# Turning the softmax of an attention layer: TensorE transposes against transfers between SBUF quarters and a 32x32 block transpose

## The chip, the core and the metric

The kernel runs on one core of a Trainium2 chip. The metric is the device time of one execution in microseconds (us). A core has TensorE (PE in the profile, with its weight loads as PEld), VectorE (DVE), ScalarE (ACT), GpSimd (POOL) and SyncE (SP), whose queue issues most of the transfers. Each engine takes its instructions strictly in the order in which they stand in its queue.

## The reference, cut to what matters

The program is a graph layer followed by a transformer block with gated mixtures in its attention, on N = 1250 nodes of D = 1024 features, H = 16 heads of P = 64, E = 8 experts of which 2 are chosen. All is float32.

```python
x = x + gnn(layernorm(x), edges, W, b)
z = layernorm(x)
q = rope(einsum('bsd,hdp->bhsp', z, Wq));  k = rope(einsum('bsd,hdp->bhsp', z, Wk))
gv = gate(z, Wsel_v);                      go = gate(z, Wsel_o)
v   = einsum('bsd,bhse,hedp->bhsp', z, gv, Wv)
att = softmax(einsum('bhsp,bhtp->bhst', q, k) / sqrt(P), axis=-1)
o   = einsum('bhst,bhtp->bhsp', att, v)
s1  = layernorm(z + einsum('bhsp,bhse,hepd->bsd', o, go, Wo))
x   = x + layernorm(s1 + relu(s1 @ W1 + b1) @ W2 + b2)
```

The einsum for o sums over the keys t. TensorE sums over partitions, so the attention weights, which come out of the softmax with queries on partitions and keys along the row, have to be turned: keys onto partitions.

## The kernel before, in words

float32 products are made from split operands: `hi` is the operand rounded to a matmul type (a cast on ACT), `lo` the rest (a subtraction on DVE or POOL), and `dot` (L137) adds hi*hi, hi*lo and lo*hi, three matmuls. Weights are read by `weights` (L119): a 128x1024 block into one of two `w_raw` buffers, cast on ACT (L127), rest on POOL (L129), into a ring of five pairs of `w_hi` and `w_lo` during the attention.

The kernel runs through five stages. The graph layer ends near 320 us. `queries_keys` (L558) makes q and k for head after head, about 365 to 600 us, and writes them to DRAM tensors `kq_d` (L594, L596), from buffers of which there are two per part. Then `values` and `attention` run side by side until about 1925 us; `outputs` runs beside the last head's attention until about 2125 us and alone until about 3000 us; `feed_forward` ends the program.

`values` (L704) makes v of one head in 10 tiles of 125 nodes. A tile is 4 steps of 6 matmuls of 512 columns, then on DVE a product with the gate (L717) and a sum over experts (L720), a cast on ACT (L722) and a rest on POOL (L723). The four weight blocks of a head serve one step each: step 1 of every tile uses block 0, step 4 block 3. A block of the next head can be cast only when a pair of the ring is free, which for blocks 1 to 3 is after the same head's last tile has used block 0, 1 or 2.

`attention` (L617) works on chunks of 256 queries, 5 chunks a head, 80 in all; a chunk has two tiles of 128 queries. `softmax` (L622) of a tile: six matmuls into three PSUM banks `s` (one buffer, so the next tile's scores wait until this one's exponentials are made), the maximum over the row on DVE (L637), three exponentials on ACT with sums of their rows (L642), sum, reciprocal and a product with 1/sum on DVE (L645 to L647). `split` (L650), five times a chunk: four TensorE transposes against the identity into a PSUM bank (L655), a cast (L657) and a rest (L659). `product` (L664), five times a chunk: four matmuls with v (L670), all 20 of a chunk summed in one bank. `outputs` (L729) reads o and the output gate (L736, L741) and multiplies by Wo.

The generators are interleaved by hand: after each step of `values` one step of `attention` follows (L834 to L838), and the order on TensorE is kept as written (`manual_schedule`, L832). On the other engines the order is set when the program is built, by a planner that places instructions by its own estimate of when they could start. On the chip the queues follow that order whatever the real times are.

Of the kernel before, what the change touches and what calls it, by code (L numbers as in the profile page):

```python
# [22 lines left out]
N = 1250  # L23
# [13 lines left out]
CUT = NZ * KT  # L37
# [33 lines left out]
def gnn_ffn_kernel(  # L71
# [31 lines left out]
    o_d = [dram.tile([P, N], F32, name=f"o_d{j}") for j in range(NP)]  # L103
    g_d = dram.tile([P, N], F32, name="g_d")
# [61 lines left out]
    def transposed(hi, lo, c0, y, psum_tile):  # L166

        for half in range(2):
            p = psum_tile([P, 4, KT])
            for k in range(4):  # L170
                d0 = (4 * half + k) * P
                nc.tensor.transpose(p[:, k, :], y[:, d0 : d0 + P], ident[:KT, :KT])
            to = (slice(None), slice(4 * half, 4 * half + 4), slice(c0, c0 + KT))
            nc.scalar.copy(hi[to], p)
            nc.vector.tensor_tensor(lo[to], p, hi[to].bitcast(F32), ALU.subtract)
# [8 lines left out]
    with ExitStack() as gctx:  # L184
# [16 lines left out]
        with ExitStack() as bctx:  # L201
# [3 lines left out]
            with tc.tile_pool(name="ring1t", bufs=6) as r1:  # L205
                ring += [r1] * 6

                def prepare(t):
# [10 lines left out]
                    transposed(yh, yl, 0, y[:KT], lambda shape: ps.tile(shape, F32, name="tr2", bufs=2))  # L219
# [274 lines left out]
        zT = [[zpool.tile([P, ND, CUT], F32R, name=f"zT0{k}") for k in range(2)]]  # L494
        for t in range(2, NT):
            new = sums([t])
            if t - 2 < NZ:
                transposed(zT[0][0], zT[0][1], KT * (t - 2), zs.pop(0)[:KT], side_bank)
                zs += new
# [5 lines left out]
    def z_of(t, d):  # L505

        k = t if t < NZ else t - NZ
        return [part[:, d, KT * k : KT * (k + 1)] for part in zT[t >= NZ]]

    def rest_of_z():  # L510

        for t in range(NZ, NT):
            z = raws[0].tile([P, D], F32, name="w_raw")[:KT]
            move(z, z_d[t])
            transposed(zT[1][0], zT[1][1], KT * (t - NZ), z, side_bank)
# [3 lines left out]
    def gates(wpool, tmp):  # L519
# [5 lines left out]
        wide = [KT, 2 * H, NX]  # L525
        order = first_wins[:KT, None, :].to_broadcast(wide)

        def pick(chosen, v, m):

            nc.vector.tensor_reduce(m, v, AX.X, ALU.max)  # L530
# [5 lines left out]
        for t in range(NT):  # L536
            p = side_bank([KT, 2 * P])
# [3 lines left out]
            s, a, b, c = (tmp.tile([KT, 2 * H, NX], F32, name=k) for k in ("s", "a", "b", "chosen"))  # L541
            m = tmp.tile([KT, 2 * H], F32, name="m")
# [5 lines left out]
            nc.vector.tensor_tensor(gate_v[:KT, t, :].rearrange("p (h e) -> p h e", h=H), s[:, :H, :], c[:, :H, :],  # L548
                                    ALU.mult)
            nc.vector.tensor_tensor(a[:, H:, :], s[:, H:, :], c[:, H:, :], ALU.mult)  # L550
            pg = psums[-1].tile([P, KT], F32, name="po", bufs=1)
            nc.tensor.transpose(pg, a[:, H:, :].rearrange("p h e -> p (h e)"), ident[:KT, :KT])
            nc.scalar.copy(gT[:, KT * t : KT * (t + 1)], pg)
# [4 lines left out]
    def queries_keys(tab, work):  # L558
# [9 lines left out]
        chunks = [(0, 0, CUT), (1, 0, 376), (1, 376, N - CUT - 376)]  # L568
# [3 lines left out]
        for h, k in pieces:  # L572
# [19 lines left out]
            if k == 2:  # L592
                for j, part in enumerate((hi.bitcast(F32), lo.bitcast(F32))):
                    nc.sync.dma_start(kq_d[h][HD * j : HD * (j + 1), 0, :], part[HD:])  # L594
# [13 lines left out]
    with tc.tile_pool(name="qktab", bufs=1) as tab, tc.tile_pool(name="qkwork", bufs=2) as work, \  # L608
            tc.tile_pool(name="gatet", bufs=2) as tmp:
        turns, rest = queries_keys(tab, work), rest_of_z()  # L610
        interleave(islice(turns, 2), rest, 1, 1 / 3)
        interleave(turns, gates(tab, tmp), 1, 3)

# [3 lines left out]
    def attention(pool):  # L617


        keys, made = {}, {}  # L620

        def softmax(h, c, i):  # L622
# [5 lines left out]
            q = pool.tile([P, 2, P], F32R, name="q", bufs=4)  # L628
# [8 lines left out]
            nc.vector.tensor_reduce(most, s[:, :, :KW], AX.XY, ALU.max, negate=True)  # L637
            p = pool.tile([P, N], F32, name="p", bufs=5)
            parts = pool.tile([P, 3], F32, name="parts", bufs=4)
            for k, k0 in enumerate(starts):  # L640
                n = KW if k == 2 else KW - 2
                nc.scalar.activation(p[:, k0 : k0 + n], s[:, k, :n], AF.Exp, bias=most,  # L642
                                     accum_out=parts[:, k : k + 1])
            total = pool.tile([P, 1], F32, name="total", bufs=4)
            nc.vector.tensor_reduce(total, parts, AX.X, ALU.add)  # L645
            nc.vector.reciprocal(total, total)
            nc.vector.tensor_scalar_mul(p, p, total)  # L647
            made.setdefault((h, c), []).append(p)

        def split(h, c, k):  # L650

            t = side_bank([KT, 2, QW])
            for j in range(2):
                for i, p in enumerate(made[h, c]):
                    nc.tensor.transpose(t[:, j, P * i : P * (i + 1)], p[:, KT * (k + j) : KT * (k + j + 1)], ident)  # L655
            hi = pool.tile([KT, 2, QW], F32R, name="att_hi", bufs=3)
            nc.scalar.copy(hi, t)  # L657
            lo = pool.tile([KT, 2, QW], F32R, name="att_lo", bufs=3)
            nc.vector.tensor_tensor(lo, t, hi.bitcast(F32), ALU.subtract)  # L659
            return hi, lo  # L660

        sums = {}

        def product(h, c, k, parts):  # L664
            if k == 0:
                sums[h, c] = psums[-1].tile([P, QW], F32, name="po", bufs=1)
            po = sums[h, c]
            for j in range(2):
                for part in parts:
                    nc.tensor.matmul(po, lhsT=v_of[h][:, k + j, :], rhs=part[:, j, :],  # L670
                                     start=(k + j == 0 and part is parts[0]),
                                     stop=(k + j == NT - 1 and part is parts[1]))
            if k + 2 < NT:
                return
# [252 lines left out]
```

## Time and profile before

| | us |
|---|---|
| runs shown (3) | 3124.57, 3132.06, 3143.47; median 3132.06 |
| the profiled execution's own time | 3137.92 |
| its span | 3136.1 |
| PE busy | 3023.9 (96%) |
| PEld, DVE, ACT, POOL busy | 2554.4, 1957.2, 1098.1, 702.2 |
| granted TensorE clock | 0.985 |

The span lies 1.8 us under that execution's time. A row of the groups gives line, engine, operation, what is written and read, count, then busy time and mean duration of one in ns, then the idle time of the engine before these instructions and what ended it. A row of the timeline gives start and length in us, engine, line and operation. Matmuls overlap in the pipeline: the step from one start to the next is what a matmul costs TensorE, and it is shorter than its recorded length.

### The profile page before, as it was taken

Reading aid. Unit: us, or ns where it says so; the run is one execution under the profiler, and the core shown is the slowest. Engines: PE = TensorE matmul, PEld = TensorE weight load, DVE = VectorE, ACT = ScalarE, POOL = GpSimd, SP = SyncE. Lnnn points to the kernel's source line nnn. Section 1 sums busy time; section 2 is a strip of 40 time slices with the busy share of each in tenths; the row PEclk is TensorE's granted clock in tenths of the full one; section 3 lists DMA queues with packets and bytes.
Section 4 is the critical chain, followed back from the end, with each engine's and each line's share of the span. In section 5 each row is a group of like instructions: output and inputs, shape, how many; then the busy total and the mean of one; then the engine's idle time right before and its main releaser. Section 6 shows DMA issues by size and latency. Waiting matters only on the chain. (4 is left out here: it accounts for less than half of the span.)

```text
span 3136.1 us, 41143 instructions
## 1 busy us (share of the span) xinstructions
PE 3023.9 (96%) x15618; PEld 2554.4 (81%) x15618; DVE 1957.2 (62%) x3477; ACT 1098.1 (35%) x2472; POOL 702.2 (22%) x570
## 2 busy tenths in 40 slices
PE   6989899999999999999999999899999999999998
PEld 5777889888888888888888888787777777777787
DVE  7965687566666666666666666664444444444685
ACT  5762323234444444444444444431112112111222
POOL 2000334322222122222212222202112112112223
PEclk9999999999999999999999999999999999999999
DMA  3116555612221121222112122434333333333212
GB/s 111 60 41 190 167 142 160 167 43 52 54 55 37 42 52 47 54 55 53 43 39 53 46 54 54 102 94 123 106 85 98 96 85 103 90 82 109 75 41 92
DMA packets 151825, 254.86 MB, mean 81 GB/s; under 512 B 14521, under 2 KB 111801, under 8 KB 151458
## 3 DMA queue, kind: packets, MB, share of 16 engines
q1 hardware_dynamic: 103934, 210.68, 23.9%
q0 software_dynamic: 45824, 31.22, 5.2%
q10 hardware_dynamic: 1860, 10.24, 1.1%
q8 instruction: 124, 2.03, 0.3%
q14 instruction: 83, 0.68, 0.1%
HBM read 200.25 MB, written 56.96 MB: 82 GB/s over the span
## 5 line engine op out<-in xcount | busy, mean ns | idle before, releaser
L129 POOL TENSOR_TENSOR w_lo<-w_raw,w_hi 128x1024 fp32r<-128x1024 f32 x148 | 372.3, 2525 | 1078.0 <-ACT w_hi L127 1069.6
L141 PE MATMUL mm<-w_hi,go_lo 128*125 128x512 f32 x1280 | 507.6, 399 | 24.6 <-DVE go_lo L750 24.5
L139 PE MATMUL mm<-w_hi,go_hi 128*125 128x512 f32 x1280 | 509.5, 398 | 8.8 <-ACT go_hi L748 7.9
L139 PE MATMUL mm<-w_hi,zT 128*125 128x512 f32 x1280 | 508.4, 397 | 4.6 <-ACT raw L584 4.6
L140 PE MATMUL mm<-w_lo,go_hi 128*125 128x512 f32 x1280 | 509.9, 398 | 0.0
L140 PE MATMUL mm<-w_lo,zT 128*125 128x512 f32 x1280 | 507.1, 396 | 0.1
L141 PE MATMUL mm<-w_hi,zT 128*125 128x512 f32 x1280 | 507.1, 396 | 0.0
L642 ACT ACTIVATE p<-s,most 128x416 f32<-128x416 f32 (+1 forms) x480 | 286.0, 605 | 332.8 <-DVE most L637 329.2
L765 DVE TENSOR_TENSOR acc<-acc,mm 125x512 f32<-125x512 f32 x320 | 217.4, 683 | 163.1 <-PE mm L141 163.1
L659 DVE TENSOR_TENSOR att_lo<-tr,att_hi 125x512 fp32r<-125x512 f32 x400 | 262.6, 685 | 88.7 <-ACT att_hi L657 88.6
L141 PEld LDWEIGHTS mm<-w_hi,go_lo 128*125 128x125 f32 x1280 | 239.9, 187 | 93.6 <-DVE go_lo L750 33.7
L748 ACT CAST go_hi<-gb 128x500 fp32r<-128x500 f32 x160 | 98.2, 614 | 602.2 <-PE mm L140 600.6
L657 ACT CAST att_hi<-tr 125x512 fp32r<-125x512 f32 x400 | 235.1, 589 | 179.0 <-PE tr L655 176.0
L139 PEld LDWEIGHTS mm<-w_hi,go_hi 128*125 128x125 f32 x1280 | 239.9, 187 | 68.3 <-ACT go_hi L748 8.2
L745 DVE TENSOR_TENSOR gb<-gb,oc 128x500 f32<-128x500 f32 x160 | 103.8, 690 | 303.0 <-DMA gb<-g_d 301.8
L141 PEld LDWEIGHTS mm<-w_hi,zT 128*125 128x125 f32 x1280 | 238.3, 186 | 60.5
L140 PEld LDWEIGHTS mm<-w_lo,go_hi 128*125 128x125 f32 x1280 | 239.7, 187 | 58.4
L637 DVE TENSOR_REDUCE most<-s 128x1 f32<-128x1254 f32 x160 | 234.2, 1464 | 81.0 <-PE s L634 80.6
L655 PEld LDWEIGHTS tr<-ident,p 128*125 128x125 f32 x1600 | 234.9, 187 | 53.6 <-DVE att_lo L659 18.6
L139 PEld LDWEIGHTS mm<-w_hi,zT 128*125 128x125 f32 x1280 | 239.1, 187 | 41.0 <-ACT raw L584 4.9
L140 PEld LDWEIGHTS mm<-w_lo,zT 128*125 128x125 f32 x1280 | 239.6, 187 | 36.5 <-POOL w_lo L129 0.4
L655 PE MATMUL tr<-ident,p 128*125 128x128 f32 x1600 | 242.0, 274 | 10.2 <-DVE att_lo L659 8.1
(201 smaller groups left out, 5166.6 us busy)
## 6 DMA issues: line engine op xcount, KB each, us to landing
gb<-g_d SPq DMA_DIRECT2D x160, 250.0 KB
w_raw<-in_wv SPq DMA_DIRECT2D x64, 512.0 KB
w_raw<-in_wo SPq DMA_DIRECT2D x64, 512.0 KB
q<-kq_d POOLq DMA_DIRECT2D x160, 128.0 KB, 2.6
kq_d<-qk_hi SPq DMA_DIRECT2D x48, 312.5 KB
kq_d<-qk_lo SPq DMA_DIRECT2D x48, 312.5 KB
k<-kq_d POOLq DMA_DIRECT2D x16, 625.0 KB, 4.4
oc<-o_d SPq DMA_DIRECT2D x80, 125.0 KB
```

Of the source, the lines that this page charges most:

```text
L129: (lo_engine or nc.gpsimd).tensor_tensor(lo, raw, hi.bitcast(F32), ALU.subtract)
L139: nc.tensor.matmul(p, lhsT=lhs[0], rhs=rhs[0], start=start, stop=False)
L140: nc.tensor.matmul(p, lhsT=lhs[0], rhs=rhs[1], start=False, stop=False)
L141: nc.tensor.matmul(p, lhsT=lhs[1], rhs=rhs[0], start=False, stop=stop)
L637: nc.vector.tensor_reduce(most, s[:, :, :KW], AX.XY, ALU.max, negate=True)
L642: nc.scalar.activation(p[:, k0 : k0 + n], s[:, k, :n], AF.Exp, bias=most, accum_out=parts[:, k : k + 1])
L655: nc.tensor.transpose(t[:, j, P * i : P * (i + 1)], p[:, KT * (k + j) : KT * (k + j + 1)], ident)
L657: nc.scalar.copy(hi, t)
L659: nc.vector.tensor_tensor(lo, t, hi.bitcast(F32), ALU.subtract)
L745: nc.vector.tensor_tensor(gb[:, :, mine], gb[:, :, mine], o[:, None, mine].to_broadcast([P, 4, KT]), ALU.mult)
L748: copied = nc.scalar.copy(hi, gb[:, :, mine])
L765: nc.vector.tensor_tensor(acc[t][:, cols], acc[t][:, cols], p, ALU.add)
```

## The change

1. `split` no longer uses TensorE. Each tile of exponentials (128 queries, 1250 keys and 30 zero columns) is cut into 16 pieces of 32 partitions by 320 columns, and 16 transfers on the SP queue carry piece (b, a) to place (a, b) of a tile `turned`. One DVE instruction then transposes every 32x32 block in place. It is issued behind the maximum of the next chunk's tile with the same number (`issue_after(found)`). Cast and rest are made from SBUF in four pieces of 128x640 per chunk on each engine, before five of 125x512 out of PSUM.
2. The keys of `kq_d` are stored in an order that makes the turned blocks contiguous: runs of 32 keys, written by 8 transfers per part instead of one (8 of 9 runs and 8 of one run a head).
3. `product` makes all 20 matmuls of a chunk at once, two chunks after its scores. Tiles of keys have 128 rows (the last 98) instead of 125, so `zT`, the gates and v are cut at 128.
4. The division by the sum leaves the softmax: `sums` writes 1/sum of a head to a DRAM tensor `r_d`, and `outputs` reads it with 2 or 4 more transfers per block of 250 queries and multiplies o by it on DVE. There `oc` has one buffer instead of two.
5. The sum over experts in `values` is three additions of halves instead of one strided reduction.
6. PSUM: four banks for `values` instead of two, none for transposes. The exponentials have one buffer for each of the two tiles of a chunk, `turned` three.

```diff
+    r_d = [dram.tile([2, NC * QW], F32, name=f"r_d{j}") for j in range(NP)]
...
-                    nc.sync.dma_start(kq_d[h][HD * j : HD * (j + 1), 0, :], part[HD:])
+                    to, n, last = kq_d[h][HD * j : HD * (j + 1), 0, :], (NT - 1) * NB, (NT - 1) * P
+                    for a in range(NA):
+                        nc.sync.dma_start(to[:, KA * a : KA * a + n].rearrange("p (b j) -> p b j", j=NB),
+                                          part[HD:, :last].rearrange("p (b a j) -> p b a j", a=NA, j=NB)[:, :, a, :])
+                        nc.sync.dma_start(to[:, KA * a + n : min(KA * (a + 1), N)],
+                                          part[HD:, last + NB * a : min(last + NB * (a + 1), N)])
...
-            total = pool.tile([P, 1], F32, name="total", bufs=4)
-            nc.vector.tensor_reduce(total, parts, AX.X, ALU.add)
-            nc.vector.reciprocal(total, total)
-            nc.vector.tensor_scalar_mul(p, p, total)
+            t = turned[n, i] = pool.tile([P, NA * KA], F32, name="turned", bufs=3)
+            for a in range(NA):
+                for b in range(NA):
+                    nc.sync.dma_start(t[NB * a : NB * (a + 1), KA * b : KA * (b + 1)],
+                                      p[NB * b : NB * (b + 1), KA * a : KA * (a + 1)])
+            return found.ins
+        def sums(h):
+            total = pool.tile([P, 2 * NC], F32, name="total", bufs=2)
+            nc.vector.tensor_reduce(total, inverse.pop(h), AX.X, ALU.add)
             nc.vector.reciprocal(total, total)
+            nc.sync.dma_start(r_d[h // 2][h % 2].rearrange("(k r) -> r k", r=P), total)
+        def split(n, i):
...
+            x = turned.pop((n, i)).rearrange("p (A k) -> p A k", A=NA)
+            for half, (hi, lo) in enumerate(parts_of[n]):
+                mine, cols = slice(NA * i, NA * (i + 1)), slice(KA // 2 * half, KA // 2 * (half + 1))
+                nc.scalar.copy(hi[:, mine], x[:, :, cols])
+                nc.vector.tensor_tensor(lo[:, mine], x[:, :, cols], hi[:, mine].bitcast(F32), ALU.subtract)
+        def product(n):
+            h, c = chunks[n]
+            po = psums[-1].tile([P, QW], F32, name="po", bufs=1)
+            for t in range(NT):
...
+                    nc.tensor.matmul(po, lhsT=v_of[h][:rows, t, :], rhs=part[:rows, :, NB * b : NB * (b + 1)],
+                                     start=(t == 0 and part is parts[0]), stop=(t == NT - 1 and part is parts[1]))
...
+        for n in range(len(chunks) + 2):
+            for i in range(2):
+                found = softmax(n, i) if n < len(chunks) else None
+                if i == 0 and n > 1:
+                    product(n - 2)
+                yield
+                if 0 < n <= len(chunks):
+                    t = turned[n - 1, i]
+                    with tc.issue_after(found) if found is not None else ExitStack():
+                        nc.vector.transpose(t, t)
+                if i == 1 and n < len(chunks) and chunks[n][1] == NC - 1:
+                    sums(chunks[n][0])
+                yield
+                if 0 < n <= len(chunks):
+                    split(n - 1, i)
+                yield
+                yield
...
-                nc.vector.tensor_reduce(v, ve.rearrange("p e k -> p k e"), AX.X, ALU.add)
+                for half in (4, 2):
+                    nc.vector.tensor_tensor(ve[:, :half], ve[:, :half], ve[:, half : 2 * half], ALU.add)
+                v = pool.tile([P, HD], F32, name="v")[:n]
+                nc.vector.tensor_tensor(v, ve[:, 0], ve[:, 1], ALU.add)
...
-                    o = pool.tile([P, QB], F32, name="oc", bufs=2)
+                    o = pool.tile([P, QB], F32, name="oc", bufs=1)
+                    r = pool.tile([P, QB], F32, name="r", bufs=1)
...
+                    nc.vector.tensor_tensor(o, o, r, ALU.mult)
...
-    banks[:] = [2, 2]
+    banks[:] = [4, 0]
...
             for k, _ in enumerate(values(apool, vpool)):
-                if k >= per_head - per_chunk and k % per_chunk < 7:
-                    if k >= per_head or k % per_chunk in (0, 3):
-                        next(heads)
+                if k >= per_head - 16:
+                    next(heads)
```

## The prediction

> **What bounds the kernel now.** First the page's busy times and groups, for the size of what goes and comes:
>
> ```profile
> PE 3023.9 (96%) x15618; PEld 2554.4 (81%) x15618; DVE 1957.2 (62%) x3477; ACT 1098.1 (35%) x2472; POOL 702.2 (22%) x570
> L659 DVE TENSOR_TENSOR att_lo<-tr,att_hi 125x512 fp32r<-125x512 f32 x400 | 262.6, 685 | 88.7 <-ACT att_hi L657 88.6
> L637 DVE TENSOR_REDUCE most<-s 128x1 f32<-128x1254 f32 x160 | 234.2, 1464 | 81.0 <-PE s L634 80.6
> L655 PE MATMUL tr<-ident,p 128*125 128x128 f32 x1600 | 242.0, 274 | 10.2 <-DVE att_lo L659 8.1
> ```
>
> TensorE is the bound, and it hardly waits for the transposes (10.2 us). The recorded 274 ns overlap, so the price of a transpose is read from the timeline of a piece of the attention, start to start:
>
> ```profile
> 1500.24 0.39 PE L141 MATMUL mm<-w_hi,zT 128*125 128x512 f32 x1
> 1500.47 0.60 PE L655 MATMUL tr<-ident,p 128*125 128x128 f32 x4
> 1500.82 0.36 PE L670 MATMUL po<-att_hi,v 125*128 125x256 f32 x1
> 1501.02 0.28 PE L670 MATMUL po<-att_lo,v 125*128 125x256 f32 x1
> 1501.38 0.40 PE L139 MATMUL mm<-w_hi,zT 128*125 128x512 f32 x1
> ```
>
> Four transposes take 0.35 us, and the four products behind them 0.56, of which the first takes 0.20 and the others 0.12. Then the stage by windows, and the transfers issued in it:
>
> ```profile
> 700.00:1900.00 1200.00, 1195.25 (x6604) 1039.82 (x6603) 800.08 (x1189) 527.28 (x1372) 300.59 (x331) 1.00 0.20 49
> q<-kq_d POOLq DMA_DIRECT2D x133, 128.0 KB, 2.6
> ```
>
> PE is busy 1195 of 1200 us. 133 loads of q are 66.5 chunks, so a chunk takes 18.05 us. Last, what the weights of the next head have to spare, around a border of heads (1562.2):
>
> ```profile
> 1558.35 1.07 ACT L127 CAST w_hi<-w_raw 128x1024 fp32r<-128x1024 f32 x1
> 1559.50 2.41 POOL L129 TENSOR_TENSOR w_lo<-w_raw,w_hi 128x1024 fp32r<-128x1024 f32 x1 [0.17 <-ACT w_hi L127]
> 1567.08 0.40 PE L139 MATMUL mm<-w_hi,zT 128*125 128x512 f32 x1
> ```
>
> The third weight block of the new head is complete at 1561.9 and needed at 1567.1: 5 us ahead.
>
> **What TensorE is spared.** Removed are 400 groups of four transposes, 400 x 0.35 = 140 us. The 20 products of a chunk stand together: 0.20 + 19 x 0.12 = 2.48 us for 5 x 0.56 = 2.80, over 80 chunks 26 us. A chunk's TensorE work is then 8 steps of 1.39 (1553.27 to 1554.65 for six matmuls), two score groups of 1.15 (1508.80 to 1509.95) and the products: 11.1 + 2.3 + 2.5 = 15.9 to 16.0 us. Tiles of 128 rows cost nothing more: the matmuls are as many and stream as many columns. Sum: -166 us, if nothing new is waited for.
>
> **Busy time of the others.** DVE loses the product with 1/sum (160 x 885 ns = 142 us) and 160 small sums and reciprocals (51). It gains 160 block transposes. No row shows one; the nearest is the shuffle of rotary halves, 583 ns for 374 columns and 723 for 500, a line that gives 1.59 us for 1280, 254 us in all; the ends are 1.4 (the step of 0.98 ns per column between the additions of 128 and 256 columns, plus 0.16) and 2.9 (the longest that a DVE operation of this case took beside POOL, row of gb). The rests are 320 x 0.82 instead of 400 x 0.685 (262 for 263), the sum over experts 160 x (0.41 + 0.285 + 0.22) instead of 160 x 1.07 (-25), o times 1/sum 80 x 0.41 = 33. That is about +70 us of 1957, spread; ACT's casts stay at 235. Neither becomes the bound by its busy time. The Trainium skill, VectorE: DVE Perf Modes, section The three transpose paths, gives 311 ns for the DVE to turn 128x128 of bf16. Ten such make an estimate of 3.1 us a tile, and by it DVE would gain another 240 us of busy time and wait more; the shuffle row of this chip is nearer in form, and I go by it.
>
> **The transfers.** 2560 are added on SP. The nearest rows:
>
> ```profile
> L680 SPq DMA_DIRECT2D o_d<-o x80: 445/446/546, 680.5 to 2121.5; - x80
> L741 SPq DMA_DIRECT2D gb<-g_d x160: 573/593/1548, 2017.0 to 2969.1; - x160
> ```
>
> A transfer of 40 KB, 32 rows, should issue like o_d (64 rows out of SBUF), 0.45 and 0.05 between: 32 a chunk take 16.0 us, with o_d and weights 16.8. By the weight loads (0.33) it is 13, by gb 21.4. Landing was 2.6 us for 128 KB. A tile's 16 are through 8 + 2.6 = 10.6 us after its last exponential; its block transpose stands behind a maximum 16 us later, and the buffer is written again later still. So the transfers are hidden; SP is the next bound, not yet the first. Also hidden: once a head `sums` writes 1280 single numbers, 80 packets per engine, 2.3 us at the 29 ns found below; and q, now with two buffers, loads in 2.6 us behind the scores of two tiles before. The Trainium skill, DMA: Bandwidth & Descriptors, section Rules for kernel authors, speaks against this: under 64 KB one pays mostly overhead, and the section Anatomy of one DMA, on transfers issued by GpSimd, sets about 2.0 us of fixed cost for each. One at a time, that is an estimate of 32 x 2.1 = 67 us a chunk; eight in flight, which is how the semaphores of the changed kernel are dealt out, 8.4 us. q's 2.6 us of landing agrees with the fixed cost; only issue is serial.
>
> **The new order on ACT and DVE.** This decides. The order of the changed kernel's ACT queue at a border of heads (`p1`, `p0` are the exponentials of the second and first tile of a chunk):
>
> ```
> L672 p1  | L758 cast of v, tile 8 | L672 p1 | L758 cast of v, tile 9 | L672 p1
> L696 att_hi x2 | L672 p0 x3 | L711 o | L696 att_hi x2
> L132 w_hi block 2 | L132 w_hi block 3 | L758 v | L132 w_hi (next head's block 0)
> ```
>
> (a) In 36 second tiles of 160 the last exponential stands behind the cast of a v tile whose matmuls run after these scores. From that tile's last matmul: product with the gate starts at 0.19 (1507.38 to 1507.57), it and three additions 1.75, cast 0.3, exponential and its sum 0.8: 3.05. TensorE meanwhile has one step, 1.39, and then the next scores, whose banks are still being read: 1.7 us of waiting. The block transpose (0.19 + 1.75 + 1.6 = 3.5) and cast (4.3) follow, and in 30 of the 36 DVE has the next maximum (4.45 to 5.9) ahead of the rest, ready at 6.8; the products should start at 4.25. Another 2.4 us. In the other 6 the rest comes first, 0.75. Sum 30 x 4.1 + 6 x 2.45 = 138 us.
>
> (b) At 15 borders the casts of blocks 2 and 3 stand behind p0 and the att_hi casts. From the end of the scores: maximum 0.2 to 1.67, exponentials to 3.6, products (late as in (a)) to 5.0, copy of o to 5.5, two att_hi to 6.95, block 2 to 8.0, its rest on POOL (2.41) to 10.5. TensorE is through step 2 at 6.4 and waits 3.9; block 3 comes 2.4 later, a step lasts 1.39: 1.0 more. Where the rest goes ahead of the maximum (7 borders) it is 6.6. 8 x 4.9 + 7 x 6.6 = 85 us. Block 2's load, now behind 16 transfers of p1, lands before its cast, just.
>
> Behind these waits on ACT and DVE stand exponentials, gate products and casts, counted above. Both prices rest on durations seen; below they could be nil if real starts differ from the built order's logic, which only a shift of TensorE by several us would do.
>
> **q and k stage.** Per head 8 transfers of 9x64 runs of 128 B and 8 small ones replace 2. No row has such short packets. From k (625 KB, 4.4 us) and q (128 KB, 2.6) landing, a packet of 512 B takes 29 ns of an engine: (4.4 - 2.6) us for 32 KB more. 36 per engine are 1.04 us; a head 8.3 + 1.0, four q writes of 1.3, weights 1.7, completions 0.6: 16.8 against 15.4 us a head (366.5 to 597.1 for 15). +20 us. Ends: nothing; or 57 ns, what q's packets show in the queue table (5.2% of 16 engines over 45824), 26 us a head, +160.
>
> **Outputs.** `oc` with one buffer and 1/sum wait on DVE for landing, some 3 us each 11 us; five banks hold two to three blocks of 2.8 us, which covers it. Without that cover 80 x 2 us. The extra tile of z and this: +8, range 0 to 100.
>
> **Sum.** 3137.9 - 166 + 138 + 85 + 20 + 8 = 3223 for the profiled execution, which is 5.9 over the median: 3217.
>
> **Rivals.** *Covered (faster):* casts and loads find room, TensorE stays the bound, (a) and (b) shrink to a few us: 3137.9 - 166 + 28 = 3000, in the median's terms 2994. For it: DVE 67% and ACT 44% busy in the stage. Against: queues are in order, and the chains above hold however idle the engine is. The sign turns where (a) and (b) fall under 138 us together, 1.7 a chunk. *SP as bound:* at gb's issue time a chunk is 21.4 us against 15.9 + 223/77 = 18.8: 77 x 2.6 = +200 on the forecast, 3415; it begins at 0.51 us an issue. Against: fewer descriptors than gb's. *Short packets:* 57 ns, 3357. *No change:* stalls and savings cancel within 16 us.
>
> **How the numbers follow.** Forecast 0.55 (own range 3130 to 3310: (a) and (b) at 60 to 140%); covered 0.25; SP or packets 0.20. A measurement tells 0.5%, 16 us, from no change. Of the forecast's mass 0.48 lies above 3148 and the rest within, of covered 0.24 below 3116: slower 0.68, same 0.07, faster 0.25. The range runs from 3000, among the covered cases, to 3390, short of SP's bound.
>
> **What would show it.** Right: L655 gone, PE idle before the scores (ended by ACT) some 60 us, before the products (ended by DVE) some 75, before matmuls with the third and fourth weight block (ended by POOL or ACT) some 85; a chunk near 18.9 us. Wrong: PE busy 99% between 700 and 1900 (covered); exponentials or block transposes waiting for `turned` transfers (SP); ACT or POOL waiting for kq_d writes before 600 us (packets). What would make it wrong most simply is a block transpose far from 1.6 us.

## The result, and the profile after

The changed kernel takes 3784.09 us (median of four, 3780.9 to 3788.8) against 3134.45 of the kernel before (3124.57 to 3143.47): a ratio of 1.2075, with a 95% interval of 1.2035 to 1.2115. The forecast was 3217 us with a range to 3390, so the direction was right and the size far off; the reason for the direction was another, as shown below. The profiled execution has a span of 3779.1 us, the kernel before 3136.1; the sums below are made between these two.

Three stretches can be cut at two instructions that both kernels have: the first load of q, and the last write of o to DRAM. The attention lies between them, with the values of the next head inside it.

| stretch | before, us | after, us | difference | forecast |
|---|---|---|---|---|
| start to first load of q | 607.9 | 707.3 | +99 | +20 |
| first load of q to last write of o | 1513.6 | 2001.5 | +488 | +57 |
| last write of o to the end | 1014.6 | 1070.3 | +56 | +8 |
| sum | 3136.1 | 3779.1 | +643 | +85 |

The page of the changed kernel, first the busy times, then groups with their idle time before them and what ended it:

```profile
PE 3041.6 (80%) x14018; PEld 2494.4 (66%) x14018; DVE 2064.4 (55%) x3513; ACT 1112.7 (29%) x2394; POOL 666.5 (18%) x570
...
L144 PE MATMUL mm<-w_hi,zT 128*128 128x512 f32 (+1 forms) x1280 | 529.9, 414 | 218.5 <-ACT w_hi L132 213.9
...
L672 ACT ACTIVATE p<-s,most 128x416 f32<-128x416 f32 (+1 forms) x480 | 289.6, 607 | 665.9 <-DMA turned<-p 437.4
...
L727 DVE STREAM_TRANSPOSE turned<-turned 128x1280 f32<-128x1280 f32 x160 | 241.3, 1508 | 331.1 <-DMA turned<-p 314.1
```

No engine is the bound any more: TensorE fell from 96% to 80%. ACT's exponentials and DVE's block transposes wait for the moves between quarters (`turned<-p`), 437 and 314 us, and TensorE waits for weights, 214 us. That is what the prediction named as the sign of the rival "SP as bound". Next the queue that issues the moves: first one line of the view by tile (minimum, median and maximum in ns), then SP's timeline (start, duration, how many in a row).

```profile
L677 SPq DMA_DIRECT2D turned<-p x2560: 507/588/1775, 718.0 to 2665.9; - x197
```

```profile
1494.02 1.03 SPq L128 DMA_DIRECT2D w_raw<-in_wv  x2
1500.39 20.62 SPq L677 DMA_DIRECT2D turned<-p  x32
1521.11 0.54 SPq L715 DMA_DIRECT2D o_d<-o  x1
1521.74 21.00 SPq L677 DMA_DIRECT2D turned<-p  x32
1542.84 0.54 SPq L715 DMA_DIRECT2D o_d<-o  x1
1543.47 10.04 SPq L677 DMA_DIRECT2D turned<-p  x16
1553.61 0.53 SPq L686 DMA_DIRECT2D r_d<-total  x1
1554.25 16.85 SPq L677 DMA_DIRECT2D turned<-p  x16
```

A chunk's 32 moves take 20.6 to 21.0 us, and SP goes from one chunk to the next without a pause: 21.35 us from 1500.39 to 1521.74. A chunk of TensorE's work is under 16 us. The gaps between the writes of o say the same over the whole stage: a median of 22.2 us, and two longer ones of 27 to 29 us in each head of five. One of these is seen at 1553.61: behind the write of the reciprocals, sixteen moves take 16.85 us in place of 10.0. At 1495 SP stands still for 5.3 us, since the exponentials whose result it has to move are late. Why they are late is seen a little before, at a border of heads (one line each of SP, ACT and TensorE):

```profile
1481.86 1.00 SPq L128 DMA_DIRECT2D w_raw<-in_wv  x2
```

```profile
1485.66 1.04 ACT L132 CAST w_hi<-w_raw 128x1024 fp32r<-128x1024 f32 x1 [10.32 <-DMA w_raw<-in_wv]
```

```profile
1486.75 0.79 PE L144 MATMUL mm<-w_hi,zT 128*128 128x512 f32 x1 [14.99 <-ACT w_hi L132]
```

Two weight blocks of the new head are issued only at 1481.86, as moves stand before them in SP's queue. ACT waits 10.3 us to cast the first, and TensorE stands 15 us for the cast.

The same 2560 durations sorted by the time since the issue before them: the 2496 that follow another within 0.2 us have a median of 588 ns and 44 ns of gap, 0.632 us from start to start; the 32 that follow after 3 us or more have 512. The issue of such a move costs more right behind another than alone.

### The profile page after: what moved, and what is told of

Its sections match the earlier page's. It is cut to its first block, busy times and chain, and to the rows that moved or that the text cites. A ratio compares the mean times of both kernels' runs of the same rounds, so it can differ in the third digit from the quotient of the medians.

```text
span 3779.1 us, 43404 instructions
## 1 busy us (share of the span) xinstructions
PE 3041.6 (80%) x14018; PEld 2494.4 (66%) x14018; DVE 2064.4 (55%) x3513; ACT 1112.7 (29%) x2394; POOL 666.5 (18%) x570
## 5 line engine op out<-in xcount | busy, mean ns | idle before, releaser
L144 PE MATMUL mm<-w_hi,zT 128*128 128x512 f32 (+1 forms) x1280 | 529.9, 414 | 218.5 <-ACT w_hi L132 213.9
L145 PE MATMUL mm<-w_lo,zT 128*128 128x512 f32 (+1 forms) x1280 | 525.1, 410 | 24.9 <-POOL w_lo L134 24.9
L146 PE MATMUL mm<-w_hi,zT 128*128 128x512 f32 (+1 forms) x1280 | 519.6, 406 | 0.0
L144 PEld LDWEIGHTS mm<-w_hi,zT 128*128 128x128 f32 (+1 forms) x1280 | 252.7, 197 | 281.0 <-ACT w_hi L132 220.5
L727 DVE STREAM_TRANSPOSE turned<-turned 128x1280 f32<-128x1280 f32 x160 | 241.3, 1508 | 331.1 <-DMA turned<-p 314.1
L751 DVE TENSOR_TENSOR ve<-mm,gate_v 128x512 f32<-128x512 f32 (+1 forms) x160 | 110.1, 688 | 427.6 <-PE mm L146 425.8
L665 PE MATMUL s<-k,q 128*128 128x418 f32 x960 | 229.1, 377 | 129.1 <-ACT p L672 128.8
L707 PE MATMUL po<-att_lo,v 128*128 128x256 f32 (+1 forms) x800 | 270.5, 358 | 76.5 <-DVE att_lo L697 76.5
L145 PEld LDWEIGHTS mm<-w_lo,zT 128*128 128x128 f32 (+1 forms) x1280 | 250.3, 196 | 89.3 <-POOL w_lo L134 34.7
L665 PEld LDWEIGHTS s<-k,q 128*128 128x128 f32 x960 | 186.4, 199 | 166.0 <-ACT p L672 153.8
L146 PEld LDWEIGHTS mm<-w_hi,zT 128*128 128x128 f32 (+1 forms) x1280 | 248.9, 194 | 63.3
L132 ACT CAST w_hi<-w_raw 128x1024 fp32r<-128x1024 f32 x154 | 159.9, 1047 | 432.4 <-DMA w_raw<-in_wv 187.7
```

What stands on the lines that cost most here:

```text
L132: nc.scalar.copy(hi, raw)
L144: nc.tensor.matmul(p, lhsT=lhs[0], rhs=rhs[0], start=start, stop=False)
L145: nc.tensor.matmul(p, lhsT=lhs[0], rhs=rhs[1], start=False, stop=False)
L146: nc.tensor.matmul(p, lhsT=lhs[1], rhs=rhs[0], start=False, stop=stop)
L665: nc.tensor.matmul(s[:, k, :KW], lhsT=q[:, part, :], rhs=keys[h][:, k0 : k0 + KW], start=(part == 0), stop=(part == 1))
L707: nc.tensor.matmul(po, lhsT=v_of[h][:rows, t, :], rhs=part[:rows, :, NB * b : NB * (b + 1)], start=(t == 0 and part is parts[0]), stop=(t ...
```

## The experiments

Two theories to begin with. *Issue:* SP's queue, at 0.63 us for each transfer, is the bound of the attention. *Landing:* exponentials and block transposes wait for the data to arrive, whatever the queue does. And beside them the forecast's own theory, that the new order on ACT and DVE costs 223 us. A time given without a ratio is that of one execution; the four of the changed kernel lie within 8 us.

**Three queues.** Of a tile's 16 moves SP issues 8, ACT 4, POOL 4.

```diff
-                    nc.sync.dma_start(t[NB * a : NB * (a + 1), KA * b : KA * (b + 1)],
+                    queue = (nc.sync, nc.scalar, nc.sync, nc.gpsimd)[b]
+                    queue.dma_start(t[NB * a : NB * (a + 1), KA * b : KA * (b + 1)],
...
```

> The 16 moves of a tile are issued by three queues: 8 by SP, 4 by ACT, 4 by POOL; same bytes, same packets, same order otherwise. Issue theory (SP's queue is the bound of the attention: 32 moves at 0.64 us from start to start, 20.6 us a chunk, and 1.1 of others): SP's share falls to 11.4 us a chunk, the chunk falls from 24.4 to 18.9 to 20.5 us, where my forecast's order waits and the issue time on ACT (5 us a chunk more) hold it; the whole 3784 - 77 x 4 to 5.5 = 3360 to 3480 us. Landing theory (the exponentials and block transposes wait for the data, not for the issue): packets and bytes are as many, so it stays within 2% of 3784.

Measured: 3624.9 us, attention 1823.9. Neither theory's number: 160 us came back where issue alone should have given 300 to 420, and landing nothing. The waits of this kernel, and one stretch of ACT's timeline, say why:

```profile
ACT o L712 <- DMA turned<-p: 262.6, 36, 14.2
PE po L708 <- DVE att_lo L698: 261.9, 80, 6.3
```

```profile
1516.18 13.09 ACTq L678 DMA_DIRECT2D turned<-p  x4
1529.31 0.37 ACT L712 COPY o<-po 64x256 f32<-64x256 f32 x1 [14.15 <-DMA turned<-p]
1529.58 1.35 ACT L697 CAST att_hi<-turned 128x640 fp32r<-128x640 f32 x2
```

ACT's moves stand in front of the copy of o and of the casts that TensorE's products need. Around the write of reciprocals (issued at 1516.4) four of them took 13.09 us. SP was relieved, and ACT got a queue that waits. So the edit did two things, and the pair below takes the second away.

**Twice the moves.** 32 moves of half the width for each tile, all on SP.

```diff
-                for b in range(NA):
-                    nc.sync.dma_start(t[NB * a : NB * (a + 1), KA * b : KA * (b + 1)],
+                for b in range(2 * NA):
+                    k = KA // 2 * (b % 2)
+                    nc.sync.dma_start(t[NB * a : NB * (a + 1), KA // 2 * b : KA // 2 * (b + 1)],
...
```

> 32 moves of half the width for each tile, all on SP: twice the issues and packets, the same bytes. Issue theory: 64 x 0.64 + 1.1 + 2.7 = 45 us a chunk, 3784 + 77 x 20.6 = 5370 us; if the issue of a narrower move is as short as the shortest seen (0.507 + 0.05), 39.5 us a chunk and 4950. Landing theory by bytes: 3784; by packets, 5% of the DMA engines' time more, under 3950.

Measured: 5477.9 us. The issue theory's first figure, 5370, is 2% short; half the bytes in a move make its issue no shorter:

```profile
L678 SPq DMA_DIRECT2D turned<-p x5120: 507/589/3423, 747.9 to 4370.8; - x197
```

The median gap between writes of o is 42.25 us, which is 64 x 0.632 + 1.8. Twice the issues take twice the time at the same bytes: the price goes by transfer and not by bytes. (The runs of contiguous data are twice as many too; the version through DRAM, below, speaks against them as the price.)

**No moves.** The exponentials write five tiles in turn and the block transpose works in place; the moves are left out, so the output is not the reference's.

```diff
-        exps = [pool.tile([P, NA * KA], F32, name=f"p{i}") for i in range(2)]
+        exps = [pool.tile([P, NA * KA], F32, name=f"p{i}") for i in range(5)]
...
-            p = exps[i]
+            p = exps[(2 * n + i) % 5]
...
-            t = turned[n, i] = pool.tile([P, NA * KA], F32, name="turned", bufs=3)
...
+            turned[n, i] = p
```

> The moves are left out: the exponentials write five tiles in turn, and the block transpose works in place on them, so the output is not the reference's. All else is as in the changed kernel, the order on each engine too. My forecast's order waits (223 us in all, a chunk of 18.9): 3784 - 77 x 5.5 = 3360, 3300 to 3420. Covered (the order waits are a few us): a chunk of 16.0 to 16.5, 3784 - 77 x 8.2 = 3150. Landing and issue theories do not differ here.

Measured: 3154.5 us, on the figure for "covered". The attention takes 1352.8 us, 160.8 less than before and 648.7 less than with the moves. Busy time of PE, PEld, DVE, ACT and POOL, the granted clock, the DMA share and GB/s in the two kernels' attention, the changed kernel first:

```profile
707.00:2709.00 2002.00, 1477.53 (x6494) 1216.93 (x6493) 1049.53 (x1430) 665.51 (x1597) 334.55 (x399) 0.84 0.39 94
```

```profile
737.00:2090.00 1353.00, 1302.31 (x6454) 1103.78 (x6453) 1047.19 (x1430) 636.40 (x1596) 362.88 (x398) 0.98 0.29 61
```

Without the moves TensorE is busy 96% of the stage. What it still waits for there, with the total, the times and the longest:

```profile
PE po L703 <- POOL v L755: 25.1, 16, 2.4
PE po L703 <- DVE att_lo L693: 15.7, 20, 3.3
...
PE s L665 <- ACT p L672: 1.8, 2, 1.5
```

All of TensorE's waits in the stage are 50 us. Scores that wait for exponentials, (a) of the forecast, are 1.8 us; products that wait for `att_lo`, its second half, 15.7.

**K in one write.** K stays in its own order, one transfer for a part instead of eight; the keys are out of order and the output is not the reference's.

```diff
-                    for a in range(NA):
-                        nc.sync.dma_start(to[:, KA * a : KA * a + n].rearrange("p (b j) -> p b j", j=NB),
...
+                    nc.sync.dma_start(to, part[HD:])
```

> K is written in its own order, one transfer for each part in place of eight, so the keys are out of order and the output is not the reference's; the attention keeps its moves. The time between the start of the q and k stage and the first load of q is 99 us longer in the changed kernel than before. If the short writes and their issue on SP make that, it goes: 3784 - 80 to 100 = 3685 to 3705. If tiles of 128 rows and the new order of z make it: no change, within 0.5% of 3784.

Measured: 3720.5 us, ratio to the kernel before 1.1857 (1.1822 to 1.1891), 64 us less than the changed kernel. The first load of q comes at 603.6 us, 104 earlier, as expected; the attention behind it took 44 us more than in the changed kernel, so less came back than expected. Some 18 of the 44 lie in the cut: where K is late, TensorE goes on with the first head's v meanwhile, so that 133 of the 3840 matmuls for v stand before the first load of q in the changed kernel, and 55 here; from that load to the first scores it takes 4.5 us there and 22.1 here. The other 26 I cannot explain.

**Reciprocals in long runs.** A 32 x 32 block transpose on DVE turns them, and four transfers of 10 runs of 128 B replace one of 1280 runs of 4 B.

```diff
-            nc.sync.dma_start(r_d[h // 2][h % 2].rearrange("(k r) -> r k", r=P), total)
+            nc.vector.transpose(whole, whole)
+            for a in range(NA):
+                nc.sync.dma_start(r_d[h // 2][h % 2].rearrange("(k a r) -> a k r", a=NA, r=NB)[a],
+                                  whole[NB * a : NB * a + 2 * NC, :])
```

> The reciprocals of a head are turned by a small block transpose on DVE and written as 40 runs of 128 B in four transfers, in place of 1280 runs of 4 B in one. In the changed kernel SP waits 83.8 us behind that write (15 times, up to 6.1 us), at a time when SP is the bound. If those waits cost the path: 3784 - 84 + 16 x 3 x 0.63 = 3730. If they only lie where SP had to wait anyway: 3784 + 30 = 3815 or the same.

Measured: 3731.2 us, as the first figure has it. The attention is 69 us shorter, and of the two long chunks in each head one is gone: the gaps of the fifth head are now 28.0, 21.7, 22.6, 22.3, 22.3. (The stretch before it was 733 us here and 707 in the changed kernel, though the code is the same up to there, and 736 to 738 in four other runs. That is not explained; the +99 of the table is the lowest of six.) SP's wait in the changed kernel, which the edit removes:

```profile
SPq L677 <- DMA r_d<-total: 83.8, 15, 6.1
```

**SP and POOL.** Half of the moves on each, none on ACT, and the reciprocals in long runs.

```diff
-                    nc.sync.dma_start(t[NB * a : NB * (a + 1), KA * b : KA * (b + 1)],
+                    (nc.sync, nc.gpsimd)[b % 2].dma_start(t[NB * a : NB * (a + 1), KA * b : KA * (b + 1)],
```

> Half of the moves of a tile on SP, half on POOL, none on ACT, and the reciprocals in long runs. Issue theory: SP 16 x 0.63 + 1.5 = 11.6 us a chunk, POOL 16 x 0.5 + 4.5 = 12.5, both below TensorE's 15.8, and no copy or cast of ACT stands behind an issue: a chunk of 16.5 to 18.9, 3784 - 77 x 5.5 to 7.9 = 3180 to 3360. If the landing of the moves holds the chunk: as with three queues, 22 us a chunk, 3600.

Measured: 3341.1 us, attention 1540.2, a median gap of 16.6 us and a mean of 18.8. The same bytes in the same packets, moved by two queues, give back 390 us against the run just before. Landing is refuted as the bound. What still lies above the kernel without moves, 187 us, was not taken apart; 45 us of it may be TensorE's wait for loads of q, which POOL issues too. The issue of a move on POOL takes 498 ns:

```profile
L680 SPq DMA_DIRECT2D turned<-p x1280: 507/582/1806, 746.5 to 2251.5; - x183
L680 POOL DMA_DIRECT2D turned<-p x1280: 498/498/544, 746.8 to 2250.1; - x183
```

**No moves and K in one write.** The edits of the two kernels above together; the output is not the reference's.

```diff
+        exps = [pool.tile([P, NA * KA], F32, name=f"p{i}") for i in range(5)]
...
+            turned[n, i] = p
...
+                    nc.sync.dma_start(to, part[HD:])
```

> Both edits together: no moves, and K in one write for each part (so the output is not the reference's). Without moves the first load of q came 129 us later than before, the attention took 160 us less, what follows it 48 us more. If the short writes of K make the whole delay: 3154 - 120 = 3035. If half of it is the new tiling of z and the gates: 3095.

Measured: 3048.5 us, near the first figure. The first load of q comes at 609.3 us, where the kernel before has 607.9: the delay of the q and k stage is K's short writes, not the tiles of 128 rows. Whether it is their issue on SP (16 + 4 transfers a head, 0.59 to 0.64 us each) or their packets was not tried; both go together. As the cut falls at the same place of TensorE's work here (54 matmuls for v before it, 52 in the kernel before), this run also gives the fairest price of the new attention without moves: 1370.0 us, 143.6 less than before.

**The kernel before with the moves.** Nothing of the new order: 16 moves of each tile of p into a spare tile that nobody reads, and two buffers for v, not three.

```diff
+            t = pool.tile([P, 4 * 312], F32, name="spare", bufs=1)
+            for a in range(4):
+                for b in range(4):
+                    nc.sync.dma_start(t[32 * a : 32 * (a + 1), 312 * b : 312 * (b + 1)],
+                                      p[32 * b : 32 * (b + 1), 312 * a : 312 * (a + 1)])
```

> The kernel before, with 16 moves of every exponential tile between quarters into a spare tile that nobody reads, on SP (and two buffers for v, as in the changed kernel, in place of three): nothing of TensorE, DVE or ACT is changed, and nobody needs the moved data. Issue theory: 32 x 0.63 + 0.6 of o + 0.3 of weights = 21.1 to 22.2 us a chunk against 18.05, through the buffers of the exponentials and the weights' loads behind them on SP: 3137 + 80 x 3.1 to 4.2 = 3385 to 3470; with the changed kernel's long chunks at the borders (a mean of 24.5 to its 22.2) too, 3137 + 80 x 6.4 = 3650. Order theory (the moves cost only through the new order on ACT and DVE, where block transposes and exponentials wait for them): under 3200.

Measured: 3597.4 us, attention 1962.6, a gap of 24.0 us between writes of o. Moves whose data nobody wants cost 460 us:

```profile
L651 SPq DMA_DIRECT2D spare<-p x2560: 507/589/1916, 644.3 to 2578.0; - x197
```

The order theory, under 3200, is out. The time lies above the plain issue figure of 3385 to 3470. The single spare tile, whose next moves have to wait for the last ones, may be most of the rest: SP waits 95.4 us in all for it, in 128 times. It was not varied. The long chunks at the borders do not appear here: TensorE waits 6.2 us for `w_hi` in this attention, against 213.9 in the changed kernel's.

**A version through DRAM.** The runs say what to do: fewer transfers. A tile goes out in one transfer from ACT's queue and comes back in four on SP; K is written in one transfer and read in the turned order; reciprocals go in long runs; 1/sum is multiplied once into the gates of a head, by a function `rescale` with 13 small transfers; there is one buffer for exponentials. Its core:

```diff
+            spread = p_d[(2 * n + i) % 4]
+            nc.scalar.dma_start(spread, p)
             for a in range(NA):
-                for b in range(NA):
-                    nc.sync.dma_start(t[NB * a : NB * (a + 1), KA * b : KA * (b + 1)],
-                                      p[NB * b : NB * (b + 1), KA * a : KA * (a + 1)])
+                nc.sync.dma_start(t[NB * a : NB * (a + 1), :].rearrange("j (b k) -> j b k", b=NA),
+                                  spread[:, KA * a : KA * (a + 1)].rearrange("(b j) k -> j b k", j=NB))
```

> A version put together from what the runs showed: a tile goes to DRAM in one transfer on ACT's queue and comes back in four on SP, 8 + 1 issues a chunk on SP in place of 33; K is written in one transfer and read back in the turned order; reciprocals in long runs; 1/sum multiplied into the gates of the head once, so that the outputs load what they loaded before; one buffer for the exponentials. Issue theory: SP some 8 us a chunk, TensorE the bound again at 15.8 to 17 us: 3154 - 110 (K) - 40 (outputs) + 0 to 60 = 3000 to 3065. Landing theory: way out, landing, way back are some 4 + 4 us in a row and the single buffer adds waits: 19 us a chunk, 3250.

Measured: 3070.6 us, ratio to the kernel before 0.9799 (0.9770 to 0.9827): 5 us above the top of what issue gives, and faster than both kernels. Its issues, the reads on SP and the write on ACT:

```profile
L686 SPq DMA_DIRECT2D turned<-p_d x640: 302/430/1567, 640.3 to 2038.9; - x160
L684 ACTq DMA_DIRECT2D p_d<-p x160: 325/326/384, 632.3 to 2033.7; - x160
```

A read of 160 KB in 128 runs is issued in 430 ns, a move of 40 KB in 32 runs in 588. They are of different kinds, but a price that rose with bytes or runs would not look so.

**Two and two.** Two buffers for exponentials, two turned tiles, in place of one and three.

```diff
-        exps = [pool.tile([P, NA * KA], F32, name=f"p{i}") for i in range(1)]
+        exps = [pool.tile([P, NA * KA], F32, name=f"p{i}") for i in range(2)]
...
-            t = turned[n, i] = pool.tile([P, NA * KA], F32, name="turned", bufs=3)
+            t = turned[n, i] = pool.tile([P, NA * KA], F32, name="turned", bufs=2)
```

> As the version through DRAM, with two buffers for the exponentials and two for the turned tiles, in place of one and three. There TensorE waited 46.0 us for scores behind exponentials that waited for the single buffer to be copied out. If the buffer is the cause: that goes, 3070 - 46 = 3025, down to 3040 if the two turned tiles bring some waits of their own. If the way back (SP waiting 408 us for the data in DRAM) holds the exponentials: 3070 or slower, as two turned tiles leave less room.

Measured: 3072.4 us, ratio 0.9776 (0.9756 to 0.9797). A miss: no gain. Scores waiting for exponentials went from 46.0 to 29.4 us, not to nothing, and products waiting for the last v tile rose from 29.5 to 37.3:

```profile
PE po L744 <- POOL v L797: 37.3, 15, 4.8
PE s L673 <- ACT p L680: 29.4, 18, 4.8
```

**Outputs as in the changed kernel.** As the last, but 1/sum multiplied in the outputs again, without the products on the gates.

```diff
-                rescale(n, i)
...
-                    o = pool.tile([P, QB], F32, name="oc", bufs=2)
+                    o = pool.tile([P, QB], F32, name="oc", bufs=1)
+                    r = pool.tile([P, QB], F32, name="r", bufs=1)
...
```

> The same, but 1/sum multiplied in the outputs, as in the changed kernel (192 more loads, 80 products, one buffer for o), and not once into the gates. From the last write of o to the end the changed kernel took 1070 us and the kernel before 1015. If 1/sum in the outputs makes these: 45 to 55 us slower than the other kernel of this pair. If the new tiles and banks make them: within 10 us of it.

Measured: 3081.3 us, ratio 0.9815 (0.9794 to 0.9835), 9 us slower than its partner: by the whole time, the second figure. By stretches it is the first: the one after the last write of o is 1061.0 us against 1019.5, so 1/sum in the outputs costs 41 us there, near what was expected; but the attention is 40 us shorter, 1408.2 against 1448.6, without the products on the gates. The work was moved and its price with it.

**Gates later.** The products on the gates a chunk later, off the border of heads, and the load of the next k too.

```diff
-            for h2 in (h, h + 1) if n == 0 else (h + 1,) if c == 2 else ():
+            for h2 in (h, h + 1) if n == 0 else (h + 1,) if c == 3 else ():
...
-            h, c = n // NC - 1, n % NC
+            h, c = n // NC - 1, n % NC - (n < NC * H)
```

> The version with two and two, with the multiplication of the gates by 1/sum put a chunk later (and the next keys' loads too), away from the border of heads, where SP has the weights to load. In the last pair the attention took 1376 us with it and 1335 without. If its 17 transfers at the border cost that, by making weights late: some 30 us back, 3040. If it costs them wherever it stands: 3072.

Measured: 3069.6 us, ratio 0.9781 (0.9757 to 0.9804), attention 1446.1. The second figure: it costs the same wherever it stands. What in the products on the gates, 13 transfers a head and one multiplication, holds the attention was not found. The DMA engines are busy 80 to 90% of the attention in these versions, against 30 to 40% in most of the changed kernel's, and there I would look first; this is the row of tenths of their busy share in 40 slices of the span, in the last version:

```profile
DMA  3115545788888888888988887983333333333213
```

## Why the prediction was wrong

**TensorE's saving was right.** The forecast had a chunk of 15.9 to 16.0 us without waits and 166 us less in all. Without moves the median gap between writes of o is 15.79 us (18.07 in the kernel before) and the attention 160.8 us shorter, waits included; 143.6 with K in one write too, where the cut is the same as before.

**The new order on ACT and DVE was mis-sized, 223 us for 50 at most.** "This decides" was said of the wrong part. (a), the 36 second tiles at 138 us, hardly shows: 1.8 us of scores behind exponentials, 15.7 of products behind `att_lo`. (b), the borders at 85 us, is a gap of 21.4 us followed by one of 12.6: 2.5 more than two of 15.8, and 15 x 2.5 = 37 us. I took the built order and let every instruction start as late as the one ahead of it allowed; in the run the waits stayed short, I think because TensorE, DVE and ACT drift against each other, which no run shows by itself. The prediction named that as what would make both prices nil, and gave the case a chance of 0.25. Had the moves been free, "covered" would have been the nearer case: 3048.5 us without K's short writes. With them it is 3154.5, no faster than before. The waits on ACT and DVE, at 50 us, do not outweigh the saving; so that "slower" came out right, for another reason than the one given, was luck.

**The step that failed is the issue time of a transfer.** "Should issue like o_d (64 rows out of SBUF), 0.45 and 0.05 between", so that 32 a chunk take 16.0 us and stay hidden. They take 20.6 and more, at medians of 0.588 and 0.044 each. The row was wrong twice. A move alone takes 0.507 to 0.512, some 0.06 more than o's write, so the kind of transfer matters. And o is written alone, with nothing issued just before it; right behind another a move takes some 0.08 more. With the first alone, 32 x (0.51 + 0.05) + 0.8 = 18.7 us, SP would just have kept pace with the forecast's chunk of 18.8. The trace of before had a better row. Its writes of k and of q's halves have the same 64 rows out of SBUF; one for k (L594) comes first, the two for q (L596) right behind it:

```profile
L596 SPq DMA_DIRECT2D kq_d<-qk_hi x32: 580/850/2077, 367.1 to 598.2; - x32
...
L594 SPq DMA_DIRECT2D kq_d<-qk_hi x16: 445/446/644, 366.5 to 597.1; - x16
```

The first, with nothing just before it, has a median of 446; the two behind it are never under 580, and their median is 850. With 0.58 and 0.05 between, a chunk is 20.2 us on SP, above the 18.8 that the forecast had for all else, and the rival's own threshold of 0.51 us is passed. Gb's 593 ns, which the forecast had as the far end, because of "fewer descriptors than gb's", was the near one. Even o's write shows it: 446 ns where it stands alone (in the run without moves), 537 in the changed kernel, behind a move.

**The rival "SP as bound" had the mechanism and half the price.** It gave 3415. Its 21.4 us a chunk is near the 22.2 measured. It lacked the chunks of 27 to 29 us, and two of 58 and 41 us in the last head, which lift the mean to 24.5, 3.1 x 80 = 250 us; the rest of the 370 is the q and k stage and the outputs, below. The reason, by the waits: here the queue that is the bound hands its delay to what stands in it. The reciprocals' write was "hidden", "2.3 us": SP waits 5.6 us behind each, and without that 53 us come back. The weights stand behind moves, so their casts and TensorE wait (214 us, page), so the next exponentials and SP itself wait (99 us of `L677 <-ACT p`). This chain is read from the trace; no run moved the weights to another queue. In the kernel before, TensorE has no such wait in the attention.

**The transfer as a fixed cost, and the block transpose.** In the Trainium skill, DMA: Bandwidth & Descriptors, section Rules for kernel authors, transfers under 64 KB are told to be joined, as one pays mostly overhead; I weighed that as a fixed cost that eight transfers in flight would hide. The rule was right and my use of it wrong: the overhead met here is in issuing, which is serial. The same section says that spreading transfers over several engines' queues adds no bandwidth and only saves issue time; here, where issue was the bound, that saving is 390 us with SP and POOL. In the Trainium skill, VectorE: DVE Perf Modes, section The three transpose paths, 311 ns for 128x128 of bf16 gave an estimate of 3.1 us a tile; the block transpose took 1.51, and the shuffle's row, by which I went, had said 1.59.

**The q and k stage was at the upper part of its bounds:** +99 for +20, with ends of 0 and 160. A head takes some 22 us and not 16.8 (the writes of 16 heads begin between 360.7 and 684.7). The forecast counted packets for the DMA engines and no issue at all, though the short writes put 20 transfers a head on SP, 12 to 13 us at the 0.59 to 0.64 us that they take. In it TensorE stands once for 57.6 us, for weights:

```profile
PE mm L144 <- ACT w_hi L132: 73.1, 3, 57.6
```

**Outputs:** +56 for +8, inside its ends. "Five banks hold two to three blocks, which covers it" did not hold. TensorE's wait for `go_lo`, the last step of the chain behind o times 1/sum, grew from 24.0 us to 58.3 in that stretch, 34 of the 56, before first:

```profile
PE mm L141 <- DVE go_lo L750: 24.0, 18, 4.1
```

```profile
PE mm L146 <- DVE go_lo L795: 58.3, 32, 5.1
```

**The sum by measured terms:** -161 for the new attention without its moves (17 of them by the cut), +649 for the moves, +99 and +56: 643 between the spans. Three of the four were off the same way, and the largest was the one set at nothing. The chances were 0.68 for slower and 0.20 for SP and packets together, and the range stopped at 3390, "short of SP's bound": it left out the very case that came.

## What to carry to other kernels

Price a transfer on the queue that issues it, from rows where one follows another at once, and ask of each queue what a chunk puts on it against what the bound leaves: here 0.63 us each, at 20 KB as at 40, and 32 of them against 16 us. Where a queue comes near the bound, count also all that stands behind in it, here weights and reciprocals. A version in which a tile goes out in one large transfer and comes back in four, in place of sixteen between quarters, takes 3070 us against 3784, and against 3135 with TensorE's transposes. Not all of the 714 us is the tile's way: K in one write gave 64 by itself, the reciprocals in long runs 53.

## What was not expected of the hardware

The same matmuls take longer when TensorE is often idle. With the same 14018 matmuls TensorE was busy 2882.1 us without moves (granted clock 0.962), 3041.6 in the changed kernel (0.894) and 3180.1 with twice the moves (0.779). The score matmuls of the last two, in ns:

```profile
L665 PE MATMUL s<-k,q x960: 346/353/717, 711.8 to 2640.7; 128*128 128x418 f32 x192
```

```profile
L665 PE MATMUL s<-k,q x960: 346/552/717, 741.5 to 4313.2; 128*128 128x418 f32 x192
```

The minimum is the same and the median is not. The Trainium skill, TensorE: Matmul & The Clock Gate, section Part 1: The HAM clock gate, tells of an array at half rate after idle time until it has been busy for a while, which agrees with a longest of 717 ns, about twice the shortest. What it cost of the end no run shows, as SP set the pace; but a share of the 80% is slow work, not more work.

The issue of a move of 20 KB takes as long as that of 40 KB (589 and 588 ns). POOL issues one in 498 ns, less than SP behind another. And a transfer of 5 KB in 1280 runs of 4 B holds up what comes after it on SP for 5.6 us on average (83.8 us in 15 times); in the run with three queues four moves on ACT's queue, around such a transfer, took 13.09 us in place of some 2.5 (4 x 0.62).
